# A GRU of 128 steps on one core: z's sigmoid by halves and seeds moved in the last five steps, fill units of steps 118 to 123 given out anew

## The chip, the core and the metric

The kernel runs on one core of one Trainium2 chip. Its time is the device time of one execution in microseconds (us); several runs are made and the median is taken. A core has a matrix engine (TensorE, PE in the profile, its weight loads shown apart as PEld), VectorE (DVE), ScalarE (ACT), GpSimd (POOL) and SyncE (SP). Each engine runs its own instructions in the order in which the program lists them, and waits on semaphores for the results of other engines.

## The reference

A GRU layer with a second matrix every fourth step, and a residual. Batch 64, T = 128 steps, width 512, all in 32-bit floats; `cond_1024` is the initial state.

```python
def step(h, inp):
    x_t, prop = inp            # prop: (t + 1) % 4 == 0 and t < T - 1
    comb = concatenate([x_t, h])
    z = sigmoid(comb @ Wz + bz)
    r = sigmoid(comb @ Wr + br)
    h_cand = tanh(concatenate([x_t, r * h]) @ Wh + bh)
    h_new = (1.0 - z) * h + z * h_cand
    h_next = where(prop, tanh(h_new @ Wp + bp), h_new)
    return h_next, h_new
out = x + ys                   # ys: h_new of all steps
```

## The kernel before

**Halves.** The batch is split into two halves of 32 rows, h = 0 and h = 1 ("first" and "second half" below). Each is a generator `half(h)` that runs over the 128 steps and yields after every piece of TensorE work; a small loop interleaves the two by the cost yielded, the second one some 700 columns behind. In one step a half has these pieces: gate R (the matmuls of `gate`, line 223 through `products`, into the bank `rec_0` or `rec_1`, left part); r's sigmoid (`crossed`, line 249, two activations into a quarter of `scratch_r`); `rh` = r times the old state (VectorE, line 845) and its transpose `rhT` (`turn`, line 252); gate Z into the left part of the bank `rec_z`; the candidate's gate H from `rhT`, into the right part of `rec_h`; tanh into `c` (line 249); `c` times z, written into z's own place (line 884); minus `keep` (line 893) gives the new state `h`, and its transpose `hT` feeds the next step.

**z.** The sigmoid of z for both halves is issued by the second half, behind its gate Z: four activations from the left part of `rec_z` into its right part, and one VectorE operation for `keep` = (z - 1) times the old state, over both halves (line 861). Only then comes, on ScalarE, the first half's tanh.

**The P gate.** In steps 3, 7, ..., 123 the new state also goes through Wp and another tanh (gate P in the right part of `rec_h`, matmuls from `wp` and `hT`); its transpose `hpT` is what the next step uses.

**Seeds.** The parts of the gates that depend on x alone are computed ahead, with the biases in them, into `cp`; `G[t]` is a view of it. `seed(i, t, h)` is a ScalarE copy (line 399) that writes them into the gate's bank, and the gate's matmuls add to them. R of step t + 1 is seeded behind the r sigmoid of step t (in steps 3 and 123 behind the P gate's tanh); H of step t + 1 behind the tanh of step t, or behind the P gate's tanh; Z of step t + 1 by the second half, behind its tanh.

**Units of x.** The x projections are computed for groups of four steps by a Strassen-like scheme that needs fewer products. A group's work is cut into batches of two products; each goes through the PSUM banks `scratch_q`, `scratch_r`, `scratch_a`, `scratch_x` and `scratch_y`, and is a list of units in one queue. A unit is one half's two matmuls for one slice of 32 of the contraction (192 columns wide, or 256 for the last steps' plain units). A batch's products come in a fixed order by bank: a, x, q, r, then x, q, r a second time, adding to what the bank holds; the second x product ("x4" below) may start only when the first one's result has been copied away (`cx`). The last unit of a product triggers what reads its bank: copies on ScalarE (`cx`, `cq`, line 509) or sums on VectorE (`mb`, lines 526 to 536). GpSimd then adds the `mb` blocks with the biases into `cp` (lines 570 and 575). The last of these, for steps 124 and 125, are `pair_left` and `pair_right`, issued at the end of step T - 7 = 121. The units of steps 126 and 127 are plain: one product, then a VectorE sum.

`fill(n, h)` takes the next n units off the queue for a half. How many is set by a tuple of three for each step: ahead of the candidate's gate, behind it, and behind the P gate. `PLACES` has the tuples for a period of eight steps, `HEAD` those of the first five steps, `TAIL` those of the last ten (118 to 127; T is 128). The order on every engine is that in which the program lists the instructions.

**The end.** At the end of a step GpSimd adds `h` to `xr`, which holds x (line 803), and SP's queue sends `xr` out every few steps (line 813). In step 127 GpSimd subtracts `keep` from `xr` (line 869), and VectorE adds `c` times z (line 887), half by half, which is sent out at once.

Of the kernel before, what the change touches and what calls it, by code (L numbers as in the profile page):

```python
# [12 lines left out]
AF = mybir.ActivationFunctionType  # L13
# [5 lines left out]
def kernel(  # L19
# [14 lines left out]
    nc = tc.nc  # L34
    B, T, D = x.shape
    H = h0.shape[1]
    P = 128
    S = 2
    V = B // S
    NQ = P // V  # L40
    J = H // NQ
# [65 lines left out]
    xr = {}  # L107
# [76 lines left out]
    )  # L184
    q_bank, r_bank, a_bank, *x_banks = range(5)
    r_ = scratch[r_bank][:, 3 * J :]

    def quarters(v):
        return v.rearrange("p n (d c j) -> p c n d j", d=2, c=2)
# [57 lines left out]
    def crossed(dst, h, i, func):  # L247
        for d in range(2):
            nc.scalar.activation(dst[ts(d, 2 * V)], gate_ps(i, h)[ts(h, 2 * V), d, :], func)  # L249
# [146 lines left out]
    def seed(i, t, h):  # L396
        if t < T:
            rows = slice(None) if i == Z else ts(h, 2 * V)
            nc.scalar.copy(  # L399
                gate_ps(i, h)[rows].rearrange("p d (c n) -> p d c n", c=C),  # L400
                G[t][rows, :, :, i, :].rearrange("p c d n -> p d c n"),
            )
# [210 lines left out]
    def pair_right(a, p1, x_, g=1):  # L613
# [6 lines left out]
    )  # L620
    HEAD = {0: (4, 6, 0), 1: (8, 6, 0), 2: (16, 12, 0), 3: (8, 6, 8), 4: (6, 8, 0)}
    TAIL = {
        T - 10: (5, 9, 0), T - 9: (1, 7, 5), T - 8: (1, 7, 0), T - 7: (1, 5, 0), T - 6: (0, 5, 0),
        T - 5: (0, 4, 3), T - 4: (0, 5, 0), T - 3: (0, 4, 0), T - 2: (0, 4, 0), T - 1: (0, 0, 0),
    }

    def both(n):
# [60 lines left out]
    def new_two(name, t):  # L688
        return shared(t, name, lambda: two.tile([P, S, J], F32, tag=name, name=f"{name}_{t}"))
# [59 lines left out]
    def behind_step(t, duo, u, h_new):  # L749
        g, j = divmod(t, Q4)  # L750
        even, odd = FIRST + 2 * duo, FIRST + 2 * duo + 1
        if t == T - 7:
            pair_left(0, 1, 2, LAST)
            pair_right(0, 1, 10, LAST)
        if t == 0:
            sum_outer(2)
            sum_outer(4)
        if t == 3:
            pair_left(1, 8, 9)
            pair_right(1, 8, 11)  # L760

        if duo >= 0:
            if u == 0 and duo >= 1 and odd - 2 < LAST:
                outer_c22(odd - 2)
                outer_c21(odd - 2)
            if even * Q4 < T:
                if u == 0:
                    sum_s34(even)
                elif u == 1:
                    outer_1(even)  # L770
                    outer_c11(even)
                    sum_raw12(odd)
                elif u == 2:
                    outer_u1(even)
                    outer_5(even)
                    sum_raw4(even)
                elif u == 3:
                    outer_c12(even)
                    outer_u2(even)
                    outer_c22(even)  # L780
                    if odd < LAST:
                        sum_s12(odd)
                elif u == 4:
                    if odd < LAST:
                        sum_s34(odd)
                    outer_c21(even)
                    if odd < LAST:
                        outer_1(odd)
                elif u == 5 and odd < LAST:
                    sum_raw4(odd)  # L790
                elif u == 6 and odd < LAST:
                    outer_u1(odd)
                    outer_c11(odd)
                elif u == 7 and odd < LAST:
                    outer_5(odd)
                    outer_c12(odd)
        if duo >= -1 and (even + 2) * Q4 < T:
            if t == 2 or (u == 6 and duo >= 0):
                sum_raw12(even + 2)
            if u == 7:  # L800
                sum_s12(even + 2)
        if t < T - 1:
            nc.gpsimd.tensor_add(xr[g][:, j], xr[g][:, j], h_new)  # L803

        n = 0
        if t >= T - CHUNK:
            n = 3 if t == T - 2 else 0
        elif j == Q4 - 1:
            n = 4
        if n:  # L810
            for h in range(S):
                for q in range(NQ):
                    nc.sync.dma_start(  # L813
                        out=out[ts(h, V), t - n + 1 : t + 1, ts(q, J)],
                        in_=xr[g][part(q), j - n + 1 : j + 1, h, :],
                    )
        if j == 1 and g >= 1 and (g + 1) * Q4 < T:
            new_xr(g + 1)
            load_x(xr[g + 1], (g + 1) * Q4, Q4)
        if t in (1, 2):  # L820
            load_xs(t + 2)
        if duo >= 0:
            if u == 3:
                load_xs(odd + 2)
            elif u == 7:
                load_xs(even + 4)

    def half(h):

        for t in range(T):  # L830
            g, j = divmod(t, Q4)
            prop = j == CHUNK - 1 and t < T - 1
            last = t == T - 1
            duo, u = divmod(t - 3, 8)
            places = HEAD.get(t) or TAIL.get(t) or PLACES[u]
            if h == 0:
                begin(t)
            h_old, hT = state[t]

            yield from gate(R, h, hT, wh[R])  # L840
            if h == 1:
                behind_r(t, duo, u)
            rh, rhT = new_two("rh", t), new_turned("rhT", "rhT", t)
            crossed(r_, h, R, AF.Sigmoid)
            nc.vector.tensor_mul(rh[:, h, :], r_, h_old[:, h, :])  # L845
            turn(rhT[:, h, :], rh[:, h, :])
            if t not in (3, T - 5):
                seed(R, t + 1, h)
            if last or t == 0:
                seed(H_, t, h)  # L850
            if h == 1:
                join(t, duo, u, 0)

            if t == 0:
                yield from fill(2 * K, h)
            yield from gate(Z, h, hT, wh[Z])
            keep = new_two("keep", t)
            if h == 1:
                for i in range(S):
                    crossed(z[:, i, :], i, Z, AF.Sigmoid)  # L860
                nc.vector.scalar_tensor_tensor(  # L861
                    out=keep, in0=z, scalar=1.0, in1=h_old, op0=ALU.subtract, op1=ALU.mult
                )
                join(t, duo, u, 1)
                if t == 1:
                    sum_raw34(1)
                    sum_inner(6, nc.gpsimd)
                if last:
                    nc.gpsimd.tensor_sub(xr[g][:, j], xr[g][:, j], keep)
                if t == 0:  # L870
                    join_x(1, 0)
                    join_x(1, 1)
                    sum_raw12(1)
                if t == 2:
                    for n in range(2, 4):
                        join_x(2, n)
            yield from fill(places[0], h)

            yield from gate(H_, h, rhT, wh[H_])
            h_new = new_two("h", t)  # L880
            cand = new_two("c", t)
            crossed(cand[:, h, :], h, H_, AF.Tanh)
            c = z[:, h, :]
            nc.vector.tensor_mul(c, cand[:, h, :], c)  # L884
            if last:
                o = xr[g][:, j, h, :]
                nc.vector.tensor_add(o, c, o)
                (nc.sync, nc.scalar)[h].dma_start(
                    out=out[ts(h, V), t, :].rearrange("b (q n) -> q b n", q=NQ), in_=o
                )  # L890
                return
            hT = new_turned("hT", "hT", t)
            nc.vector.tensor_sub(h_new[:, h, :], c, keep[:, h, :])  # L893
            turn(hT[:, h, :], h_new[:, h, :])
            if prop:
                nc.scalar.copy(gate_ps(P_, h)[ts(h, 2 * V)], bias_p[ts(h, 2 * V)])
            elif t < T - 2:
                seed(H_, t + 1, h)
            if h == 1 and t != T - 2:
                seed(Z, t + 1, 0)  # L900
            state[t + 1] = h_new, hT
            yield from fill(places[1], h)
            if h == 1 and t == T - 2:
                seed(Z, t + 1, 0)
            if prop:
                yield from gate(P_, h, hT, wp)
                h_next = new_two("hprop", t)
                hT = new_turned("hT", "hpT", t)
                crossed(h_next[:, h, :], h, P_, AF.Tanh)
                turn(hT[:, h, :], h_next[:, h, :])  # L910
                if t in (3, T - 5):
                    seed(R, t + 1, h)
                seed(H_, t + 1, h)
                state[t + 1] = h_next, hT
                yield from fill(places[2], h)
            if h == 1:
                behind_step(t, duo, u, h_new)
# [54 lines left out]
```

## Time and profile before

| | us |
|---|---|
| three runs | 1269.46, 1269.39, 1267.61 |
| median | 1269.39 |
| profiled execution, its own time | 1266.3 |
| its span on the core | 1264.5 |
| TensorE busy in the span | 1250.6 (99%) |
| VectorE, ScalarE, GpSimd busy | 803.9, 835.2, 891.1 |

The profiled execution is one execution, so a sum made from its rows is to be set against its own 1266.3 us. Rows of a timeline show the start in us from the span's start, the busy time, the engine, the line and operation, what is written from what is read, the shapes, and how many equal instructions were put together; in square brackets stands how long the engine was idle ahead of it and what ended that. A row of the waits shows who waited for whom, the sum of the waits, their number and the longest one. Lines are those of the kernel before.

The granted clock of TensorE in the profiled execution was 0.997 of full speed. From 150 to 1130 us TensorE is busy in all of 980 us; in the last 135 us it is busy for 125.56.

### The profile page before, as it was taken

To read this page: it belongs to the slowest core of one execution; us is meant where nothing else is said; L and a number is where in the kernel's file an instruction comes from. 1 tells how busy PE (TensorE), PEld (TensorE's weight loads), DVE (VectorE), ACT (ScalarE), POOL (GpSimd) and SP (SyncE) were. 2 spreads that over 40 slices of the span, in tenths; PEclk is the share of its full clock that TensorE was granted. 3 is DMA by queue.
4 is the path that set the end of the run, shared out by engine and by line. 5 is a ranking of instruction groups with operands and counts; after the bars stand their busy time and mean duration, and the time that the engine had idled before them with its cause. 6 is when DMAs were issued, how large, how long until landed. Compare 5 with 4: busy or idle time off the path is not lost.

```text
span 1264.5 us, 60718 instructions
## 1 busy us (share of the span) xinstructions
PE 1250.6 (99%) x25960; PEld 1161.0 (92%) x25960; DVE 803.9 (64%) x2165; ACT 835.2 (66%) x2685; POOL 891.1 (70%) x1032
## 2 busy tenths in 40 slices
PE   8999999999999999999999999999999999999997
PEld 4798899999999999999999999999999999999875
DVE  4665666666666666666666666666666666666544
ACT  1566666666666666666666666666666666667665
POOL 3899767777776778767778677777767787677530
PEclk9999999999999999999999999999999999999999
DMA  8301111111121110211111211111111111111010
GB/s 234 95 22 45 44 51 49 40 37 53 36 53 41 48 51 22 53 53 37 53 28 45 53 44 45 42 47 37 52 39 51 44 29 53 53 36 36 15 40 19
DMA packets 113172, 60.82 MB, mean 48 GB/s; under 512 B 12776, under 2 KB 109288, under 8 KB 112904
## 3 DMA queue, kind: packets, MB, share of 16 engines
q1 hardware_dynamic: 110532, 54.71, 16.3%
q8 instruction: 205, 3.36, 1.1%
q10 hardware_dynamic: 2116, 2.10, 0.7%
q14 instruction: 63, 0.52, 0.1%
q0 software_dynamic: 256, 0.14, 0.1%
HBM read 40.11 MB, written 16.78 MB: 45 GB/s over the span
## 4 chain that ended last, share of the span: by engine, by line
PE 94%; POOL 2%; issue 1%; DMA 1%; ACT 1%; DVE 1%; SPq 0%; ACTq 0%; POOLq 0%; DVEq 0%
PE rec L223 42%; PE rec_z L223 16%; PE scratch_r L223 13%; PE scratch_q L223 10%; PE scratch_a L223 5%; PE scratch_x L223 4%; PE scratch_y L223 4%; DMA xr<-in_x_dram 1%; POOL cp L570 1%; POOL mb L575 1%; ACT rec_z L249 0%; SPq L813 0%; POOL xr L803 0%; ACT c L249 0%; DVE rec_z L884 0%
## 5 line engine op out<-in xcount | busy, mean ns | idle before, releaser
L223 PE MATMUL rec<-wh,rhT 128*32 128x256 f32 x4096 | 375.1, 379 | 0.0
L223 PE MATMUL rec<-wh,hT 128*32 128x256 f32 x3072 | 281.2, 379 | 1.7 <-DVE hT L252 1.7
L223 PE MATMUL rec_z<-wh,hT 128*32 128x256 f32 x3072 | 281.5, 379 | 0.1
L223 PEld LDWEIGHTS rec<-wh,rhT 128*32 128x32 f32 x4096 | 249.6, 110 | 19.1 <-ACT scratch_r L249 0.5
L249 ACT ACTIVATE scratch_r<-rec 64x128 f32<-64x128 f32 x512 | 128.0, 250 | 133.9 <-PE rec L223 67.7
L399 ACT COPY rec<-cp 64x256 f32<-64x256 f32 x512 | 189.8, 371 | 21.5 <-DVE cp L437 2.0
L223 PEld LDWEIGHTS rec_z<-wh,hT 128*32 128x32 f32 x3072 | 192.1, 110 | 9.3 <-ACT rec_z L399 0.6
L223 PEld LDWEIGHTS rec<-wh,hT 128*32 128x32 f32 x3072 | 186.2, 110 | 14.6 <-ACT c L249 2.7
L249 ACT ACTIVATE rec_z<-rec_z 64x128 f32<-64x128 f32 x512 | 128.0, 250 | 97.8 <-PE rec_z L223 85.7
L249 ACT ACTIVATE c<-rec 64x128 f32<-64x128 f32 x512 | 138.9, 271 | 60.2 <-PE rec L223 48.8
L803 POOL TENSOR_TENSOR xr<-xr,h 128x256 f32<-128x256 f32 x127 | 92.9, 732 | 93.0 <-DVE h L893 93.0
L570 POOL TENSOR_TENSOR mb<-mb,mb 128x768 f32<-128x768 f32 x58 | 106.2, 1832 | 67.0 <-DVE mb L536 67.0
L570 POOL TENSOR_TENSOR cp<-mb,mb 128x768 f32<-128x768 f32 x76 | 139.0, 1829 | 8.1 <-DVE mb L536 4.4
L570 POOL TENSOR_TENSOR cp<-mb 128x768 f32<-128x768 f32 x46 | 84.3, 1832 | 56.8 <-ACT rec_z L399 55.4
L223 PE MATMUL scratch_r<-tw,s 128*32 128x192 f32 x928 | 120.9, 326 | 0.0
L509 ACT COPY cq<-scratch_q 128x384 f32<-128x384 f32 x212 | 102.0, 481 | 19.8 <-PE scratch_q L223 18.4
L526 DVE TENSOR_TENSOR cx<-scratch_r,cx 128x384 f32<-128x384 f32 x106 | 59.1, 557 | 85.8 <-PE scratch_r L223 67.9
L861 DVE SCALAR_TENSOR_TENSOR keep<-rec_z,h 128x256 f32<-128x256 f32 x96 | 40.7, 424 | 104.1 <-ACT rec_z L249 99.9
L223 PE MATMUL scratch_q<-tt,s 128*32 128x192 f32 x928 | 103.6, 326 | 0.0
L532 DVE TENSOR_TENSOR mb<-scratch_q,cx 128x384 f32<-128x384 f32 x106 | 59.0, 557 | 62.7 <-ACT cq L509 62.7
L845 DVE TENSOR_TENSOR rh<-scratch_r,h 128x128 f32<-128x128 f32 x192 | 56.0, 292 | 60.3 <-ACT scratch_r L249 60.3
L223 PE MATMUL rec<-wh,hpT 128*32 128x256 f32 x992 | 91.4, 379 | 0.1
(183 smaller groups left out, 3832.3 us busy)
## 6 DMA issues: line engine op xcount, KB each, us to landing
out_dram<-xr SPq DMA_DIRECT2D x249, 64.0 KB, 1.8
xr<-in_x_dram SPq DMA_DIRECT2D x248, 64.0 KB, 2.0
xs<-in_x_dram SPq DMA_DIRECT2D x240, 64.0 KB, 2.0
wx<-in_L_cond_Wr_dram SPq DMA_DIRECT2D x2, 512.0 KB, 5.0
wx<-in_L_cond_Wz_dram SPq DMA_DIRECT2D x1, 1024.0 KB, 7.1
wx<-in_L_cond_Wh_dram SPq DMA_DIRECT2D x1, 1024.0 KB, 8.2
wp<-in_L_cond_Wp_dram SPq DMA_DIRECT2D x4, 256.0 KB, 5.0
wh<-in_L_cond_Wr_dram SPq DMA_DIRECT2D x2, 256.0 KB, 9.9
```

The lines of the kernel that those rows point to most:

```text
L223: nc.tensor.matmul(ps[part(2 * h + c)], lhsT=left, rhs=rhs(c), start=start, stop=True, skip_group_check=True,)
L249: nc.scalar.activation(dst[ts(d, 2 * V)], gate_ps(i, h)[ts(h, 2 * V), d, :], func)
L399: nc.scalar.copy(gate_ps(i, h)[rows].rearrange("p d (c n) -> p d c n", c=C), G[t][rows, :, :, i, :].rearrange("p c d n -> p d c n"),)
L509: nc.scalar.copy(c[:, :nm], ps[:, :nm])
L526: nc.vector.tensor_add(T2[what][:, :nm], r_ps[:, :nm], T2[what][:, :nm])
L532: nc.vector.tensor_add(blocks(1, 1), runs(q_ps[:, :nm]), runs(T2[what][:, :nm]))
L570: nc.gpsimd.tensor_add(dst, a, b)
L575: nc.gpsimd.tensor_add(m, m, v.unsqueeze(1).to_broadcast([P, 2, 3 * J]))
L803: nc.gpsimd.tensor_add(xr[g][:, j], xr[g][:, j], h_new)
L845: nc.vector.tensor_mul(rh[:, h, :], r_, h_old[:, h, :])
L861: nc.vector.scalar_tensor_tensor(out=keep, in0=z, scalar=1.0, in1=h_old, op0=ALU.subtract, op1=ALU.mult)
```

## The change

Four edits, of which three act through `late`, true in the last five steps (123 to 127).

- *z by halves*: in a late step z's first half is still issued by the second half behind its gate Z: two sigmoids and a `keep` of 128 x 128. The second half's two sigmoids and its `keep` come behind that half's candidate gate, so after the first half's tanh and ahead of its own. They are written to `z_late`, the last quarter of the bank `scratch_y`, and the second half's product with `c` is written there too. In step 127 GpSimd's subtraction is split in the same way.
- *Candidate's seeds*: H of a late step is seeded behind r's sigmoid of the same step, instead of behind the tanh of the step before, or the P gate's tanh.
- *Units*: the tuples of steps 118 to 123 change. Units per half and step were 14, 13, 8, 6, 5, 7 and become 8, 14, 8, 8, 6, 9; from there on they are as before.
- *Pair sums*: `pair_left` and `pair_right` are issued at the end of step 122 instead of 121.

```diff
@@ -184,6 +184,7 @@
     )
     q_bank, r_bank, a_bank, *x_banks = range(5)
     r_ = scratch[r_bank][:, 3 * J :]
+    z_late = scratch[4][:, 3 * J :]
 
     def quarters(v):
         return v.rearrange("p n (d c j) -> p c n d j", d=2, c=2)
@@ -620,8 +621,8 @@
     )
     HEAD = {0: (4, 6, 0), 1: (8, 6, 0), 2: (16, 12, 0), 3: (8, 6, 8), 4: (6, 8, 0)}
     TAIL = {
-        T - 10: (5, 9, 0), T - 9: (1, 7, 5), T - 8: (1, 7, 0), T - 7: (1, 5, 0), T - 6: (0, 5, 0),
-        T - 5: (0, 4, 3), T - 4: (0, 5, 0), T - 3: (0, 4, 0), T - 2: (0, 4, 0), T - 1: (0, 0, 0),
+        T - 10: (1, 7, 0), T - 9: (0, 8, 6), T - 8: (0, 8, 0), T - 7: (0, 8, 0), T - 6: (0, 6, 0),
+        T - 5: (0, 4, 5), T - 4: (0, 5, 0), T - 3: (0, 4, 0), T - 2: (0, 4, 0), T - 1: (0, 0, 0),
     }
 
     def both(n):
@@ -749,7 +750,7 @@
     def behind_step(t, duo, u, h_new):
         g, j = divmod(t, Q4)
         even, odd = FIRST + 2 * duo, FIRST + 2 * duo + 1
-        if t == T - 7:
+        if t == T - 6:
             pair_left(0, 1, 2, LAST)
             pair_right(0, 1, 10, LAST)
         if t == 0:
@@ -832,6 +833,7 @@
             prop = j == CHUNK - 1 and t < T - 1
             last = t == T - 1
             duo, u = divmod(t - 3, 8)
+            late = t >= T - 5
             places = HEAD.get(t) or TAIL.get(t) or PLACES[u]
             if h == 0:
                 begin(t)
@@ -846,7 +848,7 @@
             turn(rhT[:, h, :], rh[:, h, :])
             if t not in (3, T - 5):
                 seed(R, t + 1, h)
-            if last or t == 0:
+            if late or t == 0:
                 seed(H_, t, h)
             if h == 1:
                 join(t, duo, u, 0)
@@ -855,18 +857,29 @@
                 yield from fill(2 * K, h)
             yield from gate(Z, h, hT, wh[Z])
             keep = new_two("keep", t)
-            if h == 1:
-                for i in range(S):
-                    crossed(z[:, i, :], i, Z, AF.Sigmoid)
+            z_ = (z[:, 0, :], z_late if late else z[:, 1, :])
+
+            def gate_z(part, z, keep, h_old):
+                for i in part:
+                    crossed(z_[i], i, Z, AF.Sigmoid)
                 nc.vector.scalar_tensor_tensor(
                     out=keep, in0=z, scalar=1.0, in1=h_old, op0=ALU.subtract, op1=ALU.mult
                 )
+
+            def gate_half(h, h_old=h_old):
+                gate_z((h,), z_[h], keep[:, h, :], h_old[:, h, :])
+                if last:
+                    nc.gpsimd.tensor_sub(xr[g][:, j, h, :], xr[g][:, j, h, :], keep[:, h, :])
+
+            if h == 1:
+                if late:
+                    gate_half(0)
+                else:
+                    gate_z(range(S), z, keep, h_old)
                 join(t, duo, u, 1)
                 if t == 1:
                     sum_raw34(1)
                     sum_inner(6, nc.gpsimd)
-                if last:
-                    nc.gpsimd.tensor_sub(xr[g][:, j], xr[g][:, j], keep)
                 if t == 0:
                     join_x(1, 0)
                     join_x(1, 1)
@@ -879,8 +892,10 @@
             yield from gate(H_, h, rhT, wh[H_])
             h_new = new_two("h", t)
             cand = new_two("c", t)
+            if late and h == 1:
+                gate_half(1)
             crossed(cand[:, h, :], h, H_, AF.Tanh)
-            c = z[:, h, :]
+            c = z_[h]
             nc.vector.tensor_mul(c, cand[:, h, :], c)
             if last:
                 o = xr[g][:, j, h, :]
@@ -894,7 +909,7 @@
             turn(hT[:, h, :], h_new[:, h, :])
             if prop:
                 nc.scalar.copy(gate_ps(P_, h)[ts(h, 2 * V)], bias_p[ts(h, 2 * V)])
-            elif t < T - 2:
+            elif t < T - 6:
                 seed(H_, t + 1, h)
             if h == 1 and t != T - 2:
                 seed(Z, t + 1, 0)
@@ -910,7 +925,8 @@
                 turn(hT[:, h, :], h_next[:, h, :])
                 if t in (3, T - 5):
                     seed(R, t + 1, h)
-                seed(H_, t + 1, h)
+                if not late:
+                    seed(H_, t + 1, h)
                 state[t + 1] = h_next, hT
                 yield from fill(places[2], h)
             if h == 1:
```

## Prediction

> **What bounds the kernel now.** I read the page first, then the waits of the last 135 us, then TensorE's timeline for the start of every step from 118 on, then ScalarE, VectorE and GpSimd inside one late step.
>
> ```profile
> span 1264.5 us, 60718 instructions
> PE 1250.6 (99%) x25960; PEld 1161.0 (92%) x25960; DVE 803.9 (64%) x2165; ACT 835.2 (66%) x2685; POOL 891.1 (70%) x1032
> ...
> PEld rec L223 <- ACT c L249: 3.4, 5, 1.2
> ```
>
> TensorE is busy 99% of the span. The second part is the waits between 1130 us and the end: TensorE's weight loads stand still 3.4 us there, in five waits, behind the tanh (`c`) alone. So the change can win a few microseconds, no more. The starts of the steps:
>
> ```profile
> 1172.85 0.41 PE L223 MATMUL rec<-wh,hT 128*32 128x256 f32 x2
> ...
> 1182.97 0.36 PE L223 MATMUL scratch_r<-tw,s4r 128*32 128x192 f32 x2 [0.79 <-DVE mb L535]
> ...
> 1183.64 0.39 PE L223 MATMUL rec<-wh,hT 128*32 128x256 f32 x2
> ...
> 1191.42 0.39 PE L223 MATMUL rec<-wp,hT 128*32 128x256 f32 x2
> ...
> 1194.77 0.39 PE L223 MATMUL rec<-wh,hpT 128*32 128x256 f32 x2
> ...
> 1202.55 0.39 PE L223 MATMUL rec<-wh,hT 128*32 128x256 f32 x2
> ...
> 1218.24 0.41 PE L223 MATMUL rec<-wh,hT 128*32 128x256 f32 x2
> ...
> 1225.72 0.41 PE L223 MATMUL rec<-wp,hT 128*32 128x256 f32 x2 [0.33 <-DVE hT L252]
> ...
> 1230.47 0.36 PEld L223 LDWEIGHTS rec<-wh,hpT 128*32 128x32 f32 x10 [0.38 <-ACT rec L399]
> 1237.05 0.41 PE L223 MATMUL rec<-wh,hT 128*32 128x256 f32 x2
> 1237.91 0.46 PE L223 MATMUL rec<-wh,hT 128*32 128x256 f32 x4
> 1239.63 1.11 PE L223 MATMUL rec_z<-wh,hT 128*32 128x256 f32 x16
> 1240.50 0.41 PE L223 MATMUL rec<-wh,rhT 128*32 128x256 f32 x2
> 1244.53 0.41 PE L223 MATMUL rec<-wh,hT 128*32 128x256 f32 x2 [0.33 <-DVE hT L252]
> 1245.39 0.89 PE L223 MATMUL rec<-wh,hT 128*32 128x256 f32 x12
> 1252.87 1.07 PE L223 MATMUL rec<-wh,hT 128*32 128x256 f32 x16
> ```
>
> In order these are the first halves of steps 118, 119, 119's P gate, 120, 121, 123 and 123's P gate; then the second half of step 124 (1230.47), and both halves of 125 and 126 (1237.05 and 1237.91, 1244.53 and 1245.39: 0.86 us apart) and the second of 127. A unit is four records of one half; the 16 records of z take 0.87 us (1239.63 to 1240.50) while both halves run side by side, so a half pays 0.43 us for a 256-wide unit and, by its width, 0.32 for a 192-wide one. Check: step 120 has 12 gate units and 8 narrow ones, 5.17 + 2.58 = 7.75; it took 7.78 (1194.77 to 1202.55). Steps 125 and 126 need 6.9 or less and take 7.48 each: not TensorE but the chain sets them. Here is step 125 on ScalarE (first six lines) and VectorE:
>
> ```profile
> 1239.01 0.53 ACT L249 ACTIVATE scratch_r<-rec 64x128 f32<-64x128 f32 x2 [1.13 <-PE rec L223]
> ...
> 1239.96 0.54 ACT L249 ACTIVATE scratch_r<-rec 64x128 f32<-64x128 f32 x2
> ...
> 1241.65 1.09 ACT L249 ACTIVATE rec_z<-rec_z 64x128 f32<-64x128 f32 x4 [0.75 <-PE rec_z L223]
> 1242.77 0.55 ACT L249 ACTIVATE c<-rec 64x128 f32<-64x128 f32 x2
> ...
> 1243.74 0.56 ACT L249 ACTIVATE c<-rec 64x128 f32<-64x128 f32 x2
> ...
> 1244.98 0.38 ACT L399 COPY rec_z<-cp 128x256 f32<-128x256 f32 x1 [0.28 <-DVE h L893]
> ...
> 1243.35 0.30 DVE L884 TENSOR_TENSOR rec_z<-c,rec_z 128x128 f32<-128x128 f32 x1
> 1243.75 0.29 DVE L893 TENSOR_TENSOR h<-rec_z,keep 128x128 f32<-128x128 f32 x1
> 1244.07 0.31 DVE L252 STREAM_TRANSPOSE hT<-h 128x128 f32<-128x128 f32 x1
> 1244.33 0.30 DVE L884 TENSOR_TENSOR rec_z<-c,rec_z 128x128 f32<-128x128 f32 x1
> 1244.66 0.29 DVE L893 TENSOR_TENSOR h<-rec_z,keep 128x128 f32<-128x128 f32 x1
> ```
>
> Let X be the start of the first tanh (1242.77, which is 5.72 behind the step's start). The first half of the next step starts at X + 1.76 (1244.53), the second at X + 2.62 (1245.39). The tanh waits for four sigmoids of z (1.09 us) that waited for the second half's z.
>
> **The units.** Steps 118 to 122 did 14, 13, 8, 6, 5 units per half and now do 8, 14, 8, 8, 6; step 123 goes from 7 to 9, and from there on the totals agree. Step 118 needs 5.17 + 8 x 0.32 = 7.76 and its stall at 1182.97 goes: step 119 starts at 1180.6 instead of 1183.64. But what it needs is not ready:
>
> ```profile
> 1182.84 0.54 DVE L536 TENSOR_TENSOR mb<-scratch_y,cq 128x384 f32<-128x384 f32 x1
> 1183.46 1.84 POOL L570 TENSOR_TENSOR cp<-cp,mb 128x768 f32<-128x768 f32 x1 [4.72 <-DVE mb L536]
> 1186.20 0.37 ACT L399 COPY rec<-cp 64x256 f32<-64x256 f32 x1
> 1190.39 0.56 ACT L249 ACTIVATE c<-rec 64x128 f32<-64x128 f32 x2
> 1191.64 0.38 ACT L399 COPY rec_z<-cp 128x256 f32<-128x256 f32 x1 [0.28 <-DVE h L893]
> ...
> 1152.29 0.48 ACT L509 COPY cx<-scratch_y 128x384 f32<-128x384 f32 x1
> ```
>
> The R seed of step 120 (the copy at 1186.20, issued behind 119's first r sigmoid) reads the `cp` that GpSimd finishes at 1185.30, after VectorE's `mb` at 1183.38. In the new order the three `mb` sums stand behind the second `hT` of step 118 and end at the same 1183.3, so the seed still starts at 1185.3, though the step is 3 us earlier. Behind it on ScalarE's queue stand the second r sigmoid and the z sigmoids. The second half's candidate then starts 1.35 us behind that sigmoid's start at 1185.65, at 1187.0 (estimate: the sigmoid's 0.54, then a multiply and a transpose of some 0.3 each on VectorE and 0.2 between them), against 1184.9 by TensorE alone: 2.1 lost. The second wait is new: TensorE's x4 units of batch (30, 4) now stand in step 119's fill, and need `cx` copied away, a copy that stands behind both tanh and the Z seed. Candidate ends 1188.9, second tanh 1188.95, Z seed 1.25 later (1190.39 to 1191.64), `cx` 0.40 on, 0.48 long: 1191.1. The two x4 units then put the P gate at 1191.8, while tanh and transpose alone would have allowed 1189.7. Before: 1191.42, with six narrow units (1.9 us) more done.
>
> After that: P gate and 6 units 3.66, step 120 at 1195.5; steps 120 and 121 7.76 each (8 units, above the chain's 7.48), step 122 at 1211.0; 122 chain-bound, 7.48: step 123 at 1218.5. Before: 1218.24 and two units (0.86 us) ahead. These go where TensorE waited anyway, in 123's P gate.
>
> **The last five steps.** z's sigmoids are split: two, keep, first tanh; then two more into a second bank, keep, second tanh. Kind and count on ScalarE stay. The half-wide keep has no row: between 0.29 (the sum of 128x128) and the 0.42 of the full one; I take 0.30. VectorE gets it once more, ahead of the second multiply; it ends before the tanh it stands beside, so its price is nothing.
>
> First tanh: it needs the first half's candidate, 12 units and 0.24 of drain (1.96 for four units, 1237.05 to 1239.01) behind the start: X = 5.41 instead of 5.72 where the halves are 0.86 apart. That is the gain, 0.31.
>
> Second tanh: the added wait. The sigmoid of z's second half reads the bank `rec_z`, where VectorE's multiply and subtraction of the first half work on z's first half; it is issued behind them and, in the built program, waits for that subtraction. So: subtraction ends at X + 0.98 + 0.29, sigmoids X + 1.31, 0.54 long; second tanh X + 1.88; multiply X + 2.47; subtraction + 0.33; transpose + 0.32; matmul + 0.45: X + 3.57 instead of X + 2.62. Behind the waiting sigmoid stand the second tanh, and behind that the Z seed; the second half of the next step waits for both.
>
> ```profile
> DVE mb L532 <- ACT cq L509: 62.7, 105, 1.6
> ```
>
> This row of the waits is a pair that only reads one bank: the sum at L532 needs nothing of `cq`, and still waits for its copy 105 times. The Trainium skill, "PSUM — Partial Sum Buffer", section "PSUM bank collisions raise a hardware error", asks for exactly this, a guard by bank and 32-partition quadrant, reads against reads included, and not by address. The trace agrees with 62.7 us of such waits. Guarded by address the change would come out at the sum of the first rival below; by bank, at mine.
>
> Also, a first sigmoid into `rec_z` cannot start before the second half's z is done: it starts 3.74 us behind the second half's start (1237.91 to 1241.65). So X = start of second half + 3.74 + 0.56, and the second halves follow each other by 4.30 + 3.57 = 7.87, against 7.48.
>
> Sum. Step 123: X = 1218.5 + 5.41 = 1223.9; second P gate 1227.5 (before 0.86 behind 1225.72: 1226.6). Its four units and five of fill, 3.88: second half of 124 at 1231.35 instead of 1230.47, +0.9. (Without the H seeds behind the P tanh the copies at 1230.47 no longer hold it.) 124: 7.87 against 7.44, +1.3. 125 and 126: 0.39 each, +2.1. Step 127 has no transpose: last sum at X + 2.72, 7.02 behind its second half's start against 7.20; GpSimd's two half subtractions are hidden. +1.9 us.
>
> ```profile
> 1213.39 1.83 POOL L575 TENSOR_TENSOR mb<-mb,bias_x 128x768 f32<-128x768 f32 x1 [9.84 <-DVE mb L536]
> ...
> 1218.99 1.81 POOL L570 TENSOR_TENSOR cp<-mb,mb 128x768 f32<-128x768 f32 x1
> 1260.07 0.29 DVE L887 TENSOR_TENSOR xr<-rec_z,xr 128x128 f32<-128x128 f32 x1
> ```
>
> Costed at nothing: the H seeds behind r's sigmoid push the second r sigmoid by a copy (0.40 from 1239.01's end in steps 124 to 126); it is hidden because the second half is by then 1.3 to 1.8 us behind; with halves 0.86 apart it would cost 0.34 a step. GpSimd's pair sums, four in 7.41 us (1213.39 to 1220.80), now start at 1220.3 and end at 1227.7; the Z seed of 124 waits there ahead of the P tanh, which is not due before 1228.1. SP's queue is not moved.
>
> The last sum ends 1260.36 now, so 1262.3; what follows stays. The profiled execution took 1266.3 (span 1264.5) and becomes 1268.2; the median is 1269.39, 3.1 higher, and becomes 1271.3.
>
> **Rivals.** *The second sigmoid does not hold the tanh* (no wait worth 0.9): second halves follow at about 7.1, the seeds then bite in part, and I get 0.9 us less than before: 1268.5. For: ScalarE is free there. Against: the bank row above. *Step 119 is covered* (the seed or `cx` comes in time): 3.3 less than my sum, 1268.0. Against: both waits follow from queue order. Both together: 1265, faster. *Slower*: GpSimd's pair sums miss their place. From 1228.6 on, 0.9 late, the Z seed holds the P tanh and with it both halves of 124, one for one; a start of 1.7 us later than 1220.3 makes +2.7 us, 1272.1 or more. For: nothing else is between them and the tanh. Against: GpSimd is idle 9.84 us ahead of them.
>
> **Numbers.** A measurement of this kernel tells about 0.2% (2.5 us) from no change: 1266.85 to 1271.93. My sum has chance 0.62, own range 1269.4 to 1273.3 (stalls added by eye, 0.1 to 0.4 each at a dozen places): 0.42 inside, 0.19 slower, 0.01 faster. First rival 0.15, inside; second 0.08, 0.02 of it faster; both 0.03, faster; the slower one 0.12. Faster 0.06, within 0.63, slower 0.31. Range 1267.9 to 1273.9: it holds the first two rivals and most of the slow one.
>
> **What would show it.** Right: a ScalarE seed in step 119 waiting for GpSimd's `cp` about 1.8 us; TensorE waiting about 1.4 for `cx`; the second z sigmoid starting 0.04 behind the first half's subtraction; second halves 7.9 apart in 125 to 127. Wrong: steps of 7.1, or step 120 starting before 1194.

## The result and the profile after

The changed kernel takes 1268.51 us (median of 14 runs), the kernel before 1265.90 (median of 14). The ratio is 1.0024, 95% interval 1.0014 to 1.0034: slower by 1.8 to 4.3 us, just beyond the 0.2% that the forecast took for the limit of what a measurement tells from no change.

The profiled executions differ by less (1266.3 and 1267.03 us), since they begin differently. These are the first 60 us of the kernel before, the changed one and, for later, a run of the study (the two places of z exchanged); the number behind the engines is TensorE's granted clock:

```profile
0.00:60.00 60.00, 56.12 (x1020) 36.26 (x1024) 32.18 (x84) 21.22 (x65) 35.57 (x43) 0.97 0.65 170
```

```profile
0.00:60.00 60.00, 57.15 (x1059) 42.03 (x1063) 32.46 (x85) 21.51 (x66) 35.65 (x43) 1.00 0.66 173
```

```profile
0.00:60.00 60.00, 56.91 (x950) 34.34 (x954) 29.75 (x77) 19.38 (x59) 35.05 (x43) 0.91 0.63 165
```

At 0.97, 1.00 and 0.91 step 118 starts at 1172.85, 1171.41 and 1176.11 us, although the three programs are the same up to there. The difference is made at the start: in the first 20 us the clock was 0.91, 1.00 and 0.74, and from there to 1170 us it was 1.00 in all three. At 59 us the changed kernel is 1.51 us ahead of the kernel before and the third run 3.25 us behind it, counted by the start of the same VectorE operation; at 1151 us it is 1.44 and 3.26. So everything below is measured by the **tail**: from the start of step 118's first half to the end of the last VectorE sum. It is 87.51 us before (1172.85 to 1260.36) and 89.96 after, 2.45 more, which agrees with the ratio. The page's head, and TensorE's timeline at the starts of the steps, of the changed kernel (lines are one higher than before, and more than that in the late part):

```profile
span 1265.2 us, 60723 instructions
PE 1251.2 (99%) x25960; PEld 1162.8 (92%) x25960; DVE 804.8 (64%) x2170; ACT 835.7 (66%) x2685; POOL 892.1 (71%) x1033
```

```profile
1171.41 0.41 PE L224 MATMUL rec<-wh,hT 128*32 128x256 f32 x2
...
1179.19 0.41 PE L224 MATMUL rec<-wh,hT 128*32 128x256 f32 x2
...
1184.20 0.41 PE L224 MATMUL rec<-wh,rhT 128*32 128x256 f32 x2 [1.21 <-ACT rec L400]
...
1189.66 0.36 PE L224 MATMUL scratch_x<-tt,xT 128*32 128x192 f32 x2 [1.24 <-ACT cx L510]
...
1190.34 0.39 PE L224 MATMUL rec<-wp,hT 128*32 128x256 f32 x2
...
1194.01 0.39 PE L224 MATMUL rec<-wh,hpT 128*32 128x256 f32 x2
...
1217.12 0.41 PE L224 MATMUL rec<-wh,hT 128*32 128x256 f32 x2
...
1224.30 0.41 PE L224 MATMUL rec<-wp,hT 128*32 128x256 f32 x2
...
1226.10 0.42 PE L224 MATMUL rec<-wp,hT 128*32 128x256 f32 x4 [0.32 <-DVE hT L253]
...
1228.73 0.39 PE L224 MATMUL rec<-wh,hpT 128*32 128x256 f32 x2
...
1237.86 0.42 PE L224 MATMUL rec<-wh,hT 128*32 128x256 f32 x4 [0.33 <-DVE hT L253]
1245.87 0.42 PE L224 MATMUL rec<-wh,hT 128*32 128x256 f32 x4 [0.38 <-DVE hT L253]
1253.73 0.42 PE L224 MATMUL rec<-wh,hT 128*32 128x256 f32 x4 [0.37 <-DVE hT L253]
```

They are, behind steps 118 and 119: the candidate of 119 that waits for a seed, the x4 units that wait for `cx`, 119's P gate, steps 120 and 123, both halves of 123's P gate, 124, and the second halves of 125, 126 and 127. Those follow each other by 8.01 and 7.86 us (before 7.48). ScalarE and VectorE in step 125:

```profile
1241.54 0.53 ACT L250 ACTIVATE rec_z<-rec_z 64x128 f32<-64x128 f32 x2
1242.23 0.55 ACT L250 ACTIVATE c<-rec 64x128 f32<-64x128 f32 x2 [0.16 <-PE rec L224]
1243.60 0.53 ACT L250 ACTIVATE scratch_y<-rec_z 64x128 f32<-64x128 f32 x2 [0.82 <-DVE h L908]
1244.16 0.56 ACT L250 ACTIVATE c<-rec 64x128 f32<-64x128 f32 x2
```

```profile
1242.82 0.30 DVE L899 TENSOR_TENSOR rec_z<-c,rec_z 128x128 f32<-128x128 f32 x1 [0.42 <-ACT c L250]
1243.22 0.29 DVE L908 TENSOR_TENSOR h<-rec_z,keep 128x128 f32<-128x128 f32 x1
```

The third line is the added wait: ScalarE stands idle 0.82 us ahead of z's second sigmoid, until VectorE's subtraction on the *first* half (1243.22 to 1243.51), and the second tanh stands behind it.

### The profile page after: what moved, and what is told of

It is laid out like the page before. It is cut to its first block, busy times and chain, and to the rows that moved or that the text cites. A ratio compares the mean times of both kernels' runs of the same rounds, so it can differ in the third digit from the quotient of the medians.

```text
span 1265.2 us, 60723 instructions
## 1 busy us (share of the span) xinstructions
PE 1251.2 (99%) x25960; PEld 1162.8 (92%) x25960; DVE 804.8 (64%) x2170; ACT 835.7 (66%) x2685; POOL 892.1 (71%) x1033
## 3 DMA queue, kind: packets, MB, share of 16 engines
q8 instruction: 205, 3.36, 1.1%
## 4 chain that ended last, share of the span: by engine, by line
PE 92%; POOL 3%; issue 1%; ACT 1%; DVE 1%; DMA 1%; SPq 0%; ACTq 0%; DVEq 0%; POOLq 0%
PE rec L224 42%; PE rec_z L224 15%; PE scratch_r L224 13%; PE scratch_q L224 10%; PE scratch_a L224 5%; PE scratch_x L224 4%; PE scratch_y L224 4%; POOL cp L571 1%; POOL mb L576 1%; DMA xr<-in_x_dram 1%; ACT c L250 0%; POOL mb L571 0%; SPq L814 0%; DVE h L908 0%; POOL xr L804 0%
## 5 line engine op out<-in xcount | busy, mean ns | idle before, releaser
L865 DVE SCALAR_TENSOR_TENSOR keep<-rec_z,h 128x256 f32<-128x256 f32 (+1 forms) x96 | 40.2, 419 | 101.0 <-ACT rec_z L250 95.8
L224 PE MATMUL rec<-wp,hT 128*32 128x256 f32 x992 | 91.6, 379 | 0.4 <-DVE hT L253 0.3
```

The lines of the kernel that those rows point to most:

```text
L224: nc.tensor.matmul(ps[part(2 * h + c)], lhsT=left, rhs=rhs(c), start=start, stop=True, skip_group_check=True,)
L865: nc.vector.scalar_tensor_tensor(out=keep, in0=z, scalar=1.0, in1=h_old, op0=ALU.subtract, op1=ALU.mult)
```

## The experiments

| run | what differs | tail, us | against before | ratio of times, 95% |
|---|---|---|---|---|
| kernel before | | 87.51 | | |
| changed kernel | | 89.96 | +2.45 | 1.0024, 1.0014 to 1.0034 |
| units only | before + new tuples and pair sums | 88.03 | +0.52 | 1.0001, 0.9987 to 1.0014 |
| late steps only | before + z halves + seeds | 88.78 | +1.27 | 1.0016, 1.0004 to 1.0028 |
| seeds only | before + H seeds late | 86.95 | -0.56 | 1.0000, 0.9990 to 1.0010 |
| z only | before + z halves | 88.99 | +1.48 | single run |
| z in SBUF | changed + z elsewhere | 89.95 | +2.44 | 1.0018, 1.0004 to 1.0032 |
| z in SBUF from 124 | the same, a step later | 87.63 | +0.12 | single run |
| z exchanged | changed + two places exchanged | 86.92 | -0.59 | 1.0003, 0.9991 to 1.0014 |
| z exchanged, old units | late steps only + exchanged | 85.75 | -1.76 | 0.9984, 0.9973 to 0.9995 |
| R seed | changed + one seed moved | 89.09 | +1.58 | 1.0014, 1.0002 to 1.0026 |
| units to 124 | changed + two units moved | 89.31 | +1.80 | single run |
| exchanged, two seeds | exchanged + two seeds of 119 moved | 85.35 | -2.16 | 0.9985, 0.9973 to 0.9997 |
| and units to 120 | the same + two units moved | 85.59 | -1.92 | 0.9985, 0.9972 to 0.9997 |

Each tail is that of one profiled execution. It tells tenths apart: step 123 starts 45.69 to 45.72 us behind step 118 in the six runs with the new units and step 119 otherwise unchanged, and 45.39 or 45.40 in the five with the old ones. The ratios, with the start's variation in them, do not. Step starts are given from step 118 on.

**The parts alone.** Only the diff's tuples and pair sums, or only its late steps:

```diff
+        T - 10: (1, 7, 0), T - 9: (0, 8, 6), T - 8: (0, 8, 0), T - 7: (0, 8, 0), T - 6: (0, 6, 0),
+        T - 5: (0, 4, 5), ...
-        if t == T - 7:
+        if t == T - 6:
```

> Only the new tuples of steps 118 to 123 and the pair sums at the end of step 122; z's sigmoids and the candidate's seeds as before. Measure: from the start of step 118's first half to the end of the last VectorE sum; before 87.51 us, changed kernel 89.96. My theory: the waits for the seed and for cx in step 119 are paid by the five units less that it has to do, so step 123 starts 45.7 behind step 118 (before 45.39) and the rest runs as before: 87.8 to 88.1, or +0.3 to +0.6 us. Rival, the units are what cost: 89 or more.

> Only z by halves and the candidate's seeds behind r's sigmoid in the last five steps; units and pair sums as before. Same measure. My theory: second halves follow each other by 7.9 to 8.0 us in steps 124 to 127 as in the changed kernel, and 123's P gate loses what the moved H seeds give back: 88.8 to 89.3, or +1.3 to +1.8 us on before. Rival, the late steps as such cost nothing: 87.5 or less.

The first came as expected, 88.03, the second 0.02 below its range, 88.78. With the units alone step 123 starts at 45.70 (before 45.39), and the loss is 0.52. The late steps alone cost 1.27. Apart they make 1.79, together 2.45: 0.66 belongs to neither. The late steps were split once more, into the H seeds alone and the z halves alone:

```diff
-            if last or t == 0:
+            if t >= T - 5 or t == 0:
                 seed(H_, t, h)
...
-            elif t < T - 2:
+            elif t < T - 6:
                 seed(H_, t + 1, h)
...
-                seed(H_, t + 1, h)
+                if t < T - 5:
+                    seed(H_, t + 1, h)
```

> The kernel before, with the candidate's seeds of the last five steps behind r's sigmoid and nothing else changed. Same measure. My theory: 0.3 to 0.5 us gained behind 123's P tanh; in steps 124 to 127 the seed ahead of the second r sigmoid costs 0 to 0.35 a step, the halves being 0.86 us apart: 87.0 to 88.4. Rival, the late steps' loss is the seeds' and not the bank wait's: 88.7 or more.

> Only z by halves as in the change, with the candidate's seeds, units and pair sums as before. Same measure; before 87.51, seeds alone 86.95, both 88.78. My theory: the second sigmoid's wait costs what it did, and the seeds behind the P tanh 0.3 more than in the run with both: 88.8 to 89.4. Rival, the loss needs the late seeds in the second sigmoid's queue: 88.3 or less.

The seeds gain 0.56, which is 0.05 more than the range allowed: 123's P gate takes 3.02 us to step 124 instead of 3.36, and step 124 takes 7.57 instead of 7.96. Against that, steps 125 and 126 take 7.61 and 7.56 instead of 7.48, as the seed ahead of the second r sigmoid costs about 0.1 a step. The z halves lose 1.48, with the seeds where they were, as expected. In steps 124 and 125 of that run ScalarE copies an H seed during the wait, so that it is idle for 0.36 us instead of 0.82, but the second sigmoid still starts behind the same subtraction. So the loss of the late steps is that of z; on top of the z halves the seeds gain only 0.21 (88.99 to 88.78).

**What the second sigmoid waits for.** If it is the bank `rec_z`, z has to go elsewhere. First to SBUF, which leaves the order of the work as it is:

```diff
-            z_ = (z[:, 0, :], z_late if late else z[:, 1, :])
+            if late:
+                zt = new_two("z_sb", t)
+                z_ = (zt[:, 0, :], zt[:, 1, :])
+            else:
+                z_ = (z[:, 0, :], z[:, 1, :])
```

> The changed kernel, but z's sigmoids of both halves are written to a tile in SBUF in the late steps instead of the banks rec_z and scratch_y, so that VectorE's multiply and subtraction of the first half no longer touch rec_z. Same measure. My theory (the second sigmoid waits for them by bank): it starts right behind the first tanh instead of 0.82 later, second halves follow by 7.1 to 7.3 us instead of 7.9 to 8.0, and step 127 loses no wait for the last sum: 86.3 to 87.2, below before's 87.51. Rival, the wait is hidden or the second half's candidate is late anyway: 89.5 or more.

The wait is gone (first line: the sigmoid starts behind the tanh that ended at 1245.89), and the steps 124 to 126 take 7.33, 7.33 and 7.27. But the tail is 89.95, 2.75 above the range and among the rival's values, though not for the rival's reason: 123's P gate starts at 55.56 instead of 52.89. ScalarE in step 125, then VectorE, GpSimd and TensorE in step 123 of this run:

```profile
1245.91 0.56 ACT L249 ACTIVATE z_sb<-rec_z 64x128 f32<-64x128 f32 x2
```

```profile
1224.50 1.50 DVE L902 TENSOR_TENSOR z_sb<-c,z_sb 128x128 f32<-128x128 f32 x1 [0.34 <-ACT c L249]
1226.10 1.77 DVE L911 TENSOR_TENSOR h<-z_sb,keep 128x128 f32<-128x128 f32 x1
1227.90 0.31 DVE L252 STREAM_TRANSPOSE hT<-h 128x128 f32<-128x128 f32 x1
```

```profile
1223.97 1.88 POOL L575 TENSOR_TENSOR mb<-mb,bias_x 128x768 f32<-128x768 f32 x1
1225.92 1.80 POOL L570 TENSOR_TENSOR cp<-mb,mb 128x768 f32<-128x768 f32 x1
```

```profile
1228.36 0.41 PE L223 MATMUL rec<-wp,hT 128*32 128x256 f32 x2 [2.75 <-DVE hT L252]
```

Two VectorE operations of some 0.3 us take 1.50 and 1.77, and each ends 0.15 behind a GpSimd sum (1226.00 by 1225.85, 1227.87 by 1227.72). Both read two operands from SBUF; in the kernels with z in PSUM they read one. The Trainium skill, "SBUF — State Buffer", section "Who interferes with whom", says that a VectorE instruction with two SBUF inputs contends with a GpSimd instruction that reads SBUF, and calls the ports that the two engines share an exclusive lock. The trace agrees: the GpSimd sums keep their 1.8 us, and the two VectorE operations are held until the sums end. To tell it from a VectorE that is slow on SBUF by itself, z went to SBUF only from step 124 on, where GpSimd has no pair sums:

```diff
+            if t > T - 5:
+                zt = new_two("z_sb", t)
+                z_ = (zt[:, 0, :], zt[:, 1, :])
```

> The changed kernel with z in SBUF in steps 124 to 127 only, in which GpSimd has no pair sums to do. Same measure; z in SBUF from 123 on 89.95, with 123's P gate at 55.56. My theory: the 1.5 and 1.8 us of the two VectorE operations were GpSimd's sums beside them; now none is over 0.5, the P gate starts at 52.9, and steps of 7.3 us follow: 87.0 to 87.5. Rival, VectorE is slow on two operands in SBUF by itself: operations of 1 us or more in 124 to 126 as well, 88.5 or more.

Tail 87.63, 0.13 above what was expected; P gate at 52.88. The same two operations in step 125 of this run:

```profile
1243.52 0.29 DVE L902 TENSOR_TENSOR z_sb<-c,z_sb 128x128 f32<-128x128 f32 x1 [0.33 <-ACT c L250]
1243.91 0.29 DVE L911 TENSOR_TENSOR h<-z_sb,keep 128x128 f32<-128x128 f32 x1
```

In step 123 of the same run, where z is still in PSUM, these operations took 0.29 to 0.30 us beside the same GpSimd sums; in step 127, where z is in SBUF, one that stood beside a GpSimd subtraction of 0.45 us took 0.48. So it is GpSimd's sums together with the two operands in SBUF. z may stay in PSUM if the halves change places: VectorE then works on the first half in `scratch_y`, while the second sigmoid reads and writes `rec_z`.

```diff
-            z_ = (z[:, 0, :], z_late if late else z[:, 1, :])
+            z_ = (z_late if late else z[:, 0, :], z[:, 1, :])
```

> The changed kernel, but in the late steps the first half's z is written to the quarter of scratch_y and the second half's to rec_z, so that z stays in PSUM and VectorE's work on the first half no longer touches the bank from which the second sigmoid reads. Measure as before: start of step 118 to the end of the last sum; before 87.51 us, changed kernel 89.96, z in SBUF 89.95. My theory: no 0.82 wait, second halves 7.3 us apart as with z in SBUF, and without the long VectorE operations that z in SBUF had in step 123 (1.5 and 1.8 us beside GpSimd's sums) 123's P gate starts at 52.9 as in the changed kernel: 87.3 to 87.8. Rivals: the bank wait returns at another place, 89.5 or more; the long operations come again, 89.9.

> As the run with the two places of z exchanged, with the units of steps 118 to 123 and the pair sums as before. Same measure. My theory: 123's P gate starts at 52.6, step 124 at 56.1, and the 7.3 us steps follow: 86.3 to 86.8, 0.7 to 1.2 us below before. Rival, the steps of 7.3 depend on the new tuples: 87.5 or more.

ScalarE in step 125 with the places exchanged:

```profile
1245.91 0.55 ACT L250 ACTIVATE c<-rec 64x128 f32<-64x128 f32 x2
1246.49 0.53 ACT L250 ACTIVATE rec_z<-rec_z 64x128 f32<-64x128 f32 x2
1247.09 0.56 ACT L250 ACTIVATE c<-rec 64x128 f32<-64x128 f32 x2
```

Tanh, sigmoid and tanh stand back to back; the 0.82 is gone, no VectorE operation is long, and the tail is 86.92, 3.04 less than the changed kernel's, for one line. With the units of before it is 85.75; both are 0.4 to 0.6 under what was expected. The time of the latter is below before's by 0.05 to 0.27%. Whether the two engines could have used the bank at once was not tried: the wait itself was left to the program. Each of these banks is also one tile of the program, so these runs don't tell a wait by bank from a wait by tile.

**Step 119.** The seed that waits for GpSimd's `cp`, moved behind the P gate's tanh:

```diff
-            if t not in (3, T - 5):
+            if t not in (3, T - 9, T - 5):
                 seed(R, t + 1, h)
...
-                if t in (3, T - 5):
+                if t in (3, T - 9, T - 5):
                     seed(R, t + 1, h)
```

> The changed kernel, but the R seed of step 120 is issued behind the P gate's tanh of step 119 instead of behind r's sigmoid, so that nothing on ScalarE's queue in step 119 waits for GpSimd's cp. Same measure. My theory: the second r sigmoid starts 1.8 to 2.2 us earlier, the P gate follows, the x4 units still wait about 1.2 us for cx, and all behind it moves up: 87.9 to 88.3. Rival, the time is given back at the P gate or at the pair sums: 89.5 to 90.

A miss by 0.8: the tail is 89.09. The seed's wait is gone, but of the 2.1 us that I put on it only 1.40 came back at the P gate (17.53 instead of 18.93), and step 120 returned 0.54 of them (8.32 us to step 121 instead of 7.78). ScalarE and TensorE of this run:

```profile
1183.30 0.25 ACT L250 ACTIVATE scratch_r<-rec 64x128 f32<-64x128 f32 x1 [0.42 <-DVE rh L847]
...
1196.16 0.25 ACT L250 ACTIVATE scratch_r<-rec 64x128 f32<-64x128 f32 x1 [1.15 <-DVE mb L536]
```

```profile
1189.15 0.36 PE L224 MATMUL scratch_x<-tt,xT 128*32 128x192 f32 x2 [1.57 <-ACT cx L510]
```

The second r sigmoid now waits 0.42 for the first half's `rh`, which reads the same quarter of `scratch_r`; the wait for `cx` grew from 1.24 to 1.57; and in step 120 the R seeds, now behind the P tanhs and ahead of `cq`'s copy, put off the sum that reads `scratch_r`, for which r's sigmoid waits. With the places of z exchanged, the Z seed of step 119 was moved as well, behind `cx`:

```diff
-            if h == 1 and t != T - 2:
+            if h == 1 and t not in (T - 9, T - 2):
                 seed(Z, t + 1, 0)
...
-            if h == 1 and t == T - 2:
+            if h == 1 and t in (T - 9, T - 2):
                 seed(Z, t + 1, 0)
```

> The changed kernel with the two places of z exchanged, R's seed of step 120 behind the P gate's tanh, and in step 119 the Z seed behind the units, so that the copy of cx stands ahead of it on ScalarE's queue. Same measure. My theory: 0.9 from R's seed as measured, 0.4 to 0.8 more from cx (TensorE's wait for it 0.8 to 1.2 instead of 1.57), some of it given back in step 120: 86.0 to 86.9. Rival, step 119 is bound by its own chain: 86.9 to 87.5.

```profile
1187.67 0.36 PE L224 MATMUL scratch_x<-tt,xT 128*32 128x192 f32 x2 [0.85 <-ACT cx L510]
```

The wait for `cx` is 0.85, the P gate starts at 16.82, and the tail is 85.35, the shortest of the study. That is 0.65 under what I expected for the lower end. By its time it can't be told from the run with the old units (0.9985 and 0.9984); both are below the kernel before and the changed one. One more step failed:

```diff
-        ... T - 9: (0, 8, 6), T - 8: (0, 8, 0), ...
+        ... T - 9: (0, 8, 4), T - 8: (2, 8, 0), ...
```

> As the run with the two places of z exchanged and step 119's two seeds moved, and the last two of the units behind 119's P gate given to step 120, ahead of its candidate: (0, 8, 4) and (2, 8, 0). Same measure; that run 85.35, with 120 to 121 8.33 us, where r's sigmoid waits 1.15 for an mb sum that reads its bank. My theory: the P gate stage is TensorE's (4 gate units and 6 narrow ones, 3.66) and loses 0.64; step 120 has 10 narrow units, 8.4, and no wait for the sum, so it takes the same 8.3 to 8.4: 84.7 to 84.9. Rival, the P gate stage is bound by tanh and seeds: 85.3 or more.

85.59: the P gate stage (from the P gate's start to the next step's) went from 3.67 to 3.35 and not to 3.02, the wait of 1.15 stayed where it was, and step 120 took 8.66. The rival's chain of tanh and seeds bounds half of it: the first half's seeds behind its P tanh end at 1191.51, and TensorE starts the next gate's matmuls at 1191.56, its weight loads having waited 0.51 for them.

**The 0.66 that belong to neither part.** 123's P gate takes 4.43 us to step 124 in the changed kernel, 3.88 with the units only, 3.57 with the late steps only.

```diff
-        T - 5: (0, 4, 5), T - 4: (0, 5, 0), ...
+        T - 5: (0, 4, 3), T - 4: (0, 7, 0), ...
```

> The changed kernel, but two of the five wide units behind 123's P gate are done in step 124 instead, behind its candidate. Same measure; changed kernel 89.96, 123's P gate to step 124 4.43 (3.57 with the units of before). My theory: the two units are 0.86 us of TensorE that nothing covers there, once the H seeds no longer stand behind the P tanh, and the P gate stage takes 3.57; step 124, whose second half takes 8.0, hides most of them: 89.1 to 89.5. Rival, the 4.43 are the pair sums' (the Z seed waits for them ahead of the P tanh): the stage stays at 4.3 to 4.5 and the end at 89.9 or more.

The stage takes 3.58 and the tail is 89.31, 0.65 less. So the two units are TensorE time that nothing covers there. The steps' starts show where the 0.66 lies. With the units alone the stage is 0.52 longer than before, and step 124 gives 0.30 of that back (7.66 instead of 7.96). With the late steps the units make the stage 0.86 longer, and step 124 gives nothing back (7.34 with and without them). Of the 0.66 that is 0.64. A likely reason is that the seeds behind the P tanh already held TensorE there, so that part of the two units cost nothing; no run shows it by itself.

## Why the prediction was right, and where it was not

Its direction and its range held. The likeliest case, a loss within 0.2%, was left by a hair with 1.0024: the +1.9 us of the sum are +2.45 in the traces. In absolute terms it said 1271.3 and the median is 1268.51, since the 1269.39 of three runs, on which it stood, was 3.5 above the median of 14. That 1268.51 lies beside the first rival's 1268.5 and the second's 1268.0 is an accident of that base; what tells the rivals from the sum are the waits and the tails.

From step 118 on, in us:

| | predicted | measured |
|---|---|---|
| step 119 | 7.75 | 7.78 |
| 119's P gate | 18.95 | 18.93 |
| step 120 | 22.65 | 22.60 |
| step 123 | 45.65 | 45.71 |
| 123's P gate, second half | 54.65 | 54.69 |
| second half of 125 | 66.4 | 66.45 |
| second half of 126 | 74.2 | 74.46 |
| second half of 127 | 82.1 | 82.32 |
| end of the last sum | 89.45 | 89.96 |

- *Step 119.* Both waits are there: the R seed waits 1.77 for GpSimd's `cp` (about 1.8 by the forecast), TensorE 1.24 for `cx` (about 1.4). That they were two separate prices was wrong: with the first gone, 0.7 of its 2.1 us went into other waits of the same chain. The second rival's 3.3 was probably too much as well: no run takes both waits away, but with the seed's gone and that for `cx` at 0.85, the P gate starts 2.1 earlier, and the tail is 1.57 shorter than without these two moves (86.92 to 85.35). The path that the forecast followed, the second half's, is borne out: its tanh starts 16.07 us behind step 118, by the forecast 16.10. Not foreseen was that the same seed holds TensorE too, 1.21 us ahead of the first half's candidate, whose gate lies in the bank that the seed is written to. ScalarE in step 119 of the changed kernel:

```profile
1183.78 0.37 ACT L400 COPY rec<-cp 64x256 f32<-64x256 f32 x1 [1.77 <-POOL cp L571]
```

- *The second sigmoid.* It was to wait for the first half's subtraction, by bank; it starts 0.09 behind its end (0.04 by the forecast), and two ways of giving z another place took the wait and 0.6 to 0.7 us a step away. The first rival, the case without it, was priced 2.8 below my sum; where the wait was taken away the tail fell by 3.04.
- *The seeds* were costed at nothing in the steps, and taken off 123's P gate: alone they measure about 0.1 a step, 0.34 less at the P gate, 0.39 less in step 124, and -0.56 in all.
- *The pair sums* were in time for the second half, which sets the pace, and the rival that they would hold both halves did not happen. The Z seed does wait 0.97 for them on ScalarE, ahead of the first half's P tanh; the second half's P tanh waits for TensorE alone, 0.31:

```profile
1226.33 0.38 ACT L400 COPY rec_z<-cp 128x256 f32<-128x256 f32 x1 [0.97 <-POOL cp L571]
...
1228.06 0.56 ACT L250 ACTIVATE hprop<-rec 64x128 f32<-64x128 f32 x2 [0.31 <-PE rec L224]
```

- *The last step* is the term that was mis-sized. I gave it 7.02 us from the second half's start to the end, and 7.20 before. The rows of before that I had quoted give 7.49 (1252.87 to 1260.36), so that slip took 0.29 off the gain that I credited; and it measured 7.64. Without the slip the sum would have been +1.6: that it came out nearer to the +2.45 is luck. ScalarE and VectorE in step 127 of the changed kernel:

```profile
1258.11 0.55 ACT L250 ACTIVATE c<-rec 64x128 f32<-64x128 f32 x2 [0.16 <-PE rec L224]
1259.55 0.53 ACT L250 ACTIVATE scratch_y<-rec_z 64x128 f32<-64x128 f32 x2 [0.89 <-DVE xr L902]
```

```profile
1259.16 0.29 DVE L902 TENSOR_TENSOR xr<-rec_z,xr 128x128 f32<-128x128 f32 x1 [0.17 <-DVE rec_z L899]
...
1261.08 0.29 DVE L902 TENSOR_TENSOR xr<-scratch_y,xr 128x128 f32<-128x128 f32 x1
```

The last sum reads `rec_z` as well, so the second sigmoid waits there too, 0.89 (0.82 in the steps 124 to 126). I had let the step without a transpose run free of the wait that I had found for the others: X to the end was 3.26 us, not 2.72.

## What to carry to other kernels

When two engines' work is interleaved more finely, list for each PSUM bank who reads or writes it at that moment, whatever the address: here the same two sigmoids cost 0.8 us a step or nothing, depending on which half lived in the bank from which the next one was read. Before moving such an operand to SBUF, look at what GpSimd does in that stretch. And compare single profiles from an event that both share; a start at another clock can be larger than the effect.

## What was not expected of the hardware

- The same instructions up to step 118 took 1171.17 to 1176.11 us in the profiled executions. Of the three shown above, the granted clock of the first 20 us was 1.00 in the one that took 1171.41, 0.91 in the one that took 1172.85 and 0.74 in the one that took 1176.11.
- A VectorE operation on two SBUF operands, 0.29 us alone, took 1.50 and 1.77 beside GpSimd sums of 1.8 us, while a transpose of one operand took 0.31 beside GpSimd's next addition.
